# One-hots held twice: high and low parts of a matmul's second operand stacked on 128 rows in a four-layer graph network

## The chip, the cores and the metric

The kernel runs on one core of a Trainium2 chip. The metric is the device time in microseconds (us) of one execution. TensorE (PE in the profile) multiplies, VectorE (DVE), ScalarE (ACT) and GpSimd (POOL) work elementwise, and SyncE (SP) issues the DMAs. Matmul operands are mostly of type fp32r, a reduced form of float32[...]. To keep accuracy, a float32 operand is often split into a high part (rounded to fp32r) and a low part (the rest), and both are multiplied into the same sum.

## The reference

`x` has 8 batches of 2048 nodes with 64 channels, so a tile of 128 nodes is 128 x 512 numbers. Four layers follow each other, each as `x = layernorm(x + layer(x))`: a Chebyshev graph convolution with weights per node (layer 0), a hypergraph attention (layer 1), a graph convolution with two weights (layer 2), and one with normalized adjacency (layer 3). All use the same adjacency. Layer 1 is what matters here:

```
h = x @ W
alpha = softmax(where(H.T > 0, leaky_relu(h @ a_node), NEG))
agg = alpha @ h                                  # per hyperedge (64 of them)
beta = sigmoid((h @ a_gn)[:, None] + (agg @ a_ge)[None, :])
all_he = elu(beta * h[:, None] + (1 - beta) * agg[None, :])   # every node, every edge
coefs1 = softmax(where(H > 0, attn_scores(elu(agg)), NEG))    # over the edges of a node
g = sum over edges of coefs1 * all_he
industry = (adj / deg) @ (x @ W_ind)
coefs2 = softmax of attn_scores of (industry, g);  out = their mixture
```

A node lies in few of the 64 hyperedges: one drawn for it, and each other with a chance of 3%. The kernel uses that. Instead of all 64 edges it takes, for each node, its first, second and third edge, and a fourth list for what is left over. "The agg of this node's u-th edge" is then a product of a one-hot matrix (edges x nodes) with `agg` (edges x 512).

## The kernel before

**First product** (0 to 151 us). TensorE multiplies the adjacency with `x`, high and low (L471), while the lists of layer 1 are prepared beside it by the generator `memberships` (L295). For each quarter of the nodes (512 columns) VectorE makes two tiles of one-hots. `oh01` has the one-hots of the first edge on rows 0 to 63 and of the second edge on rows 64 to 127. `oh23` has those of the third edge and of the left-over list in the same way. They are stored in DRAM (L362, L400), along with `S` (which places left-over memberships) and `pT`. The working memory of this stage is then used again by layer 0, whose loads `srow` and `et` at 149 us wait for it.

**Layer 0** (151 to about 716 us) does the second product with the adjacency and the sums over node weights.

**Layer 1, preparation** (716 to 745 us, L511 on). `pT`, `oh01`, `S` and `oh23` are loaded whole, 128 x 2048 for the one-hots, on SyncE's queue (L541 to L544). `agg` is finished; its 64 edges stand twice, on rows 0 to 63 and on rows 64 to 127. The function `halves` makes a high and a low tile of `agg + 1` (`agg_hi`, `agg_lo`) and of `-agg` (`nagg_hi`, `nagg_lo`). The last step is a reciprocal on VectorE (L614), whose result `hgr` the loop needs. The temporary tiles of this part are in a pool `fa`, which is closed after it.

**Layer 1, loop** (745 to 1058 us). Four generators do the work of a node tile in small steps:

- `units(j)` (L643) is the attention of tile j. `sx` (L649) multiplies the one-hots with sums of `agg`, two matmuls of 32 columns in plain float32; then come `S` with `hgr` (L653) and a transpose. `gp0` and `gp1` (L696) fetch the agg rows of edges 1 and 2, and of edge 3 and the left-over list. Each is four matmuls on 64 rows: u = 0 high, u = 0 low, u = 1 high, u = 1 low. VectorE works on the result in `z0` and `z1` (L706, L710, L714), then exponential (L716) and minimum and maximum (L735). `dp` (L721, L723) is for the left-over list: `S` with `h`, then two 64-row matmuls with `nagg`. The result buffer of gp exists once.
- `industry(j)` is the product of the adjacency's mask with `x @ W_ind`: 32 matmuls of 128 rows and 512 columns into one accumulator (L1353), in groups of four, each group a step `p.i`. Its 1 MB mask tile `mj` is loaded on SyncE (L1348) into one of two buffers. `dlt` (L766) reads the accumulator and frees it for the next tile's first matmul.
- `mix_and_norm(j)` mixes, with transposes (`trm`), `fc` (L801) and `df` (L810), and normalizes.
- `layer2_steps` makes layer 2's features, `u` (L866), from each finished tile; most of them run after the loop, 1058 to 1095 us.

The order is written out by hand in the string `turns` (L894): one turn holds steps of six tiles, and begins with `q.ind u.gp0 u.z0 q.dlt m.xg m.tr0`, and later has `p.i u.w0 u.gp1 v.ST p.i`. `program_order()` makes TensorE, VectorE, ScalarE and GpSimd keep that order. SyncE's order is set by a scheduler: each DMA stands in its queue and waits there for the memory that it writes, and those behind it wait too. Nodes' tiles in memory come from pools that are stacked on each other, so the address of a later pool depends on the size of earlier ones.

**Layers 2 and 3** (1095 to 1363 us). Layer 2's product `a` (L1353 as well) loads the mask tiles again, into three buffers of a new pool `mj2`; that pool opens after layer 1's pools have closed, and so lies in memory that they used.

Of the kernel before, what the change touches and what calls it, by code (L numbers as in the profile page):

```python
# [8 lines left out]
F32 = mybir.dt.float32  # L9
# [3 lines left out]
ALU = mybir.AluOpType  # L13
AX = mybir.AxisListType
# [4 lines left out]
P = 128  # L19
NT = N // P  # L20
NQ, QW = 4, 512
NP = B // 2
BC = B * C
# [23 lines left out]
def r_(ap):  # L47
    return ap.bitcast(F32R)
# [3 lines left out]
def kernel(  # L52
# [56 lines left out]
    def b_view(t2):  # L109
        return t2.rearrange("p (b c) -> p b c", b=B)  # L110
# [118 lines left out]
    def lists_flag(box, tot, pm, w, an, avc):  # L229
# [53 lines left out]
    s_row = scr.tile([1, N], F32, tag="s_row", name="s_row")  # L283
    lists = {
        k: [scr.tile(shape, F32, tag=f"{k}{q}", name=f"{k}_{q}") for q in range(NQ)]
        for k, shape in (
            ("oh01", [P, QW]), ("oh23", [P, QW]), ("S", [P, 4, P]), ("pT", [E, QW])
        )
    }
    kept_i = [  # L290
        [scr.tile([P, BC], F32, tag=f"i{j}_{k}", name=f"kept_i_{j}_{k}") for k in range(2)]
# [3 lines left out]
    def memberships(pre, ps, pm, fcw_sb, fcb_sb, fcg_sb):  # L295
# [24 lines left out]
            pre.tile([P, NT], F32, tag=k, name=k) for k in ("cnt3", "base3", "end3")  # L320
        )
        raws = {}

        def load(q):
            raws[q] = pre.tile([P, QW], F32, tag="pT_raw", name=f"pT_raw_{q}")
# [20 lines left out]
        for q in range(NQ):  # L346

            raw = raws.pop(q)
            pT = pre.tile([P, QW], F32, tag="pT", name=f"pT_{q}")
            nc.vector.tensor_scalar(r_(pT), raw, 0.0, None, op0=ALU.is_gt)  # L350
            nc.sync.dma_start(lists["pT"][q], pT[0:E])
            yield
            pf = ps.tile([P, QW], F32, tag="li", name=f"pf_{q}")
            nc.tensor.matmul(
                pf, r_(tri.rearrange("p h e -> p (h e)")), r_(pT[0:E]), start=True, stop=True
            )
            yield
            pfm = raw
            nc.vector.tensor_tensor(pfm, pf, pT, ALU.mult)
            oh01 = pre.tile([P, QW], F32, tag="oh01", name=f"oh01_{q}")  # L360
            nc.vector.tensor_scalar(r_(oh01), pfm, order01, None, op0=ALU.is_equal)
            nc.sync.dma_start(lists["oh01"][q], oh01)  # L362
            oh23 = pre.tile([P, QW], F32, tag="oh23", name=f"oh23_{q}")
            nc.vector.tensor_scalar(r_(oh23[0:64]), pfm[0:64], 3.0, None, op0=ALU.is_equal)
            if q + 1 < NQ:
                load(q + 1)
            S = pre.tile([P, 4, P], F32, tag="S", name=f"S_{q}")
            yield
            for t in range(4):
# [26 lines left out]
                yield  # L396
                nc.vector.tensor_tensor(
                    r_(oh23[64:128, cols]), sm[64:128, P:2 * P], iota[64:128, 1, :], ALU.is_equal
                )
            nc.sync.dma_start(lists["oh23"][q], oh23)  # L400
            nc.sync.dma_start(lists["S"][q], S)
            yield

# [107 lines left out]
    def layer1(  # L511
# [7 lines left out]
        l1 = stack.enter_context(tc.tile_pool(name="fl1", bufs=1))  # L519

        oh01 = l1.tile([P, N], F32, tag="oh01", name="oh01")
        oh23 = l1.tile([P, N], F32, tag="oh23", name="oh23")

        S = l1.tile([P, NT, P], F32, tag="S", name="S")

        agg_hi, agg_lo = (
            l1.tile([P, BC], F32, tag=f"agg{i}", name=f"agg_{i}") for i in range(2)
        )  # L530
# [4 lines left out]
        ext = l1.tile([P, 2, 2, B], F32, tag="ext", name="ext")  # L535

        with tc.tile_pool(name="fa", bufs=2) as fa:
            pT = fa.tile([E, N], F32, tag="pT", name="pT", bufs=1)
            for q in range(NQ):
                cols = slice(q * QW, (q + 1) * QW)  # L540
                nc.sync.dma_start(pT[:, cols], lists["pT"][q])  # L541
                nc.sync.dma_start(oh01[:, cols], lists["oh01"][q])
                nc.sync.dma_start(S[:, 4 * q:4 * q + 4, :], lists["S"][q])
                nc.sync.dma_start(oh23[:, cols], lists["oh23"][q])  # L544
            stage1 = ExitStack()
            ps_tr, ps_mm = (
                stage1.enter_context(tc.tile_pool(name=n, bufs=k, space=PSUM))
# [2 lines left out]
            with program_order():  # L550
# [2 lines left out]

                he = fa.tile([P, BC], F32, tag="xT", name="he")
                nc.scalar.activation(he, agg, AF.Exp)
                nagg_hi, nagg_lo = (
                    own.tile([P, BC], F32, tag=f"b0_{k}", name=f"nagg_{k}") for k in (11, 15)
                )

                def halves(hi, lo, f, c):  # L560
                    s = slice(0 if c else 64, P)
                    nc.vector.tensor_scalar(r_(hi[s]), agg[s], f, c, op0=ALU.mult, op1=ALU.add)
                    full = fa.tile([P, BC], F32, tag="full", name="full", bufs=1)
                    nc.vector.tensor_scalar(full[s], agg[s], f, c, op0=ALU.mult, op1=ALU.add)
                    nc.vector.tensor_tensor(r_(lo[s]), full[s], hi[s], ALU.subtract)

                nc.vector.tensor_scalar(he, he, 1.0, -1.0, op0=ALU.min, op1=ALU.add)
                nc.vector.tensor_tensor(he, he, agg, ALU.max)
# [2 lines left out]
                    transpose(tr[:, pr, :], he[:, pr * P:(pr + 1) * P])  # L571
                heT = fa.tile([P, NP * P], F32, tag="hs", name="heT", bufs=3)
                nc.scalar.copy(heT, tr.rearrange("p r c -> p (r c)"))
                halves(agg_hi, agg_lo, 1.0, 1.0)
                fc = ps_mm.tile([P, 2, QW], F32, tag="mm", name="fche")
                for h in range(2):
                    rs = slice(h * 64, (h + 1) * 64)
# [4 lines left out]
                    b_view(he), b_view(agg),  # L582
                    vecs[:, 2, :].unsqueeze(1).to_broadcast([P, B, C]), ALU.mult,
                )
                nc.gpsimd.memset(ext, 0.0)
                sp = ps_tr.tile([P, QW], F32, tag="sm", name="sep")
                for b in range(B):
                    nc.tensor.matmul(
# [12 lines left out]
                for j in range(NT):  # L601
# [4 lines left out]
                for h in range(2):  # L606
                    s = slice(h * 64, (h + 1) * 64)
                    nc.vector.tensor_reduce(ext[s, h, 0, :], b_view(he)[s], AX.X, ALU.add)
                    nc.vector.tensor_copy(ext[s, h, 1, :], ese[s])
# [31 lines left out]
        extv = ext.rearrange("p u k b -> p (u k b)")  # L641

        def units(j, dst):  # L643

            cols = slice(j * P, (j + 1) * P)
# [45 lines left out]
            for i in range(2):  # L691
                gp = ps_g.tile([P, 2, BC], F32, tag="g", name=f"gp_{j}_{i}")
                for u in range(2):
                    rs = slice(u * 64, (u + 1) * 64)
                    for part in (agg_hi, agg_lo):
                        nc.tensor.matmul(  # L696
                            gp[:, u, :], r_((oh01, oh23)[i][rs, cols]), r_(part[rs]),
                            start=part is agg_hi, stop=part is agg_lo,
                        )
# [18 lines left out]
                if i == 0:  # L718

                    dp = ps_m.tile([P, BC], F32, tag="m", name=f"dp_{j}")  # L720
                    nc.tensor.matmul(dp, S[:, j, :], h_sb[:, j, :], start=True, stop=False)  # L721
                    for part in (nagg_hi, nagg_lo):
                        nc.tensor.matmul(  # L723
                            dp, r_(oh23[64:128, cols]), r_(part[64:128]),
                            start=False, stop=part is nagg_lo,
                        )
# [1356 lines left out]
```

## Time and profile before

| | us |
|---|---|
| three runs | 1359.33, 1359.80, 1364.57 |
| median | 1359.8 |
| profiled execution | 1364.62 |
| its span in the profile | 1362.9 |

| part of the span | from | to |
|---|---|---|
| first product, with the lists | 0 | 151 |
| layer 0 | 151 | 716 |
| layer 1, preparation | 716 | 745 |
| layer 1, loop | 745 | 1058 |
| layer 2's features | 1058 | 1095 |
| layer 2 and layer 3 | 1095 | 1363 |

| in the loop, 889.39 to 906.82 us | |
|---|---|
| TensorE busy, 889.4 to 906.8 | 17.40 of 17.40 us |
| VectorE busy | 14.71 us |
| ScalarE busy | 10.84 us |
| GpSimd busy | 10.46 us |
| granted TensorE clock | 1.00 |

A line of a timeline has the start, the duration, the engine, the line of the kernel, the operation, what it writes and reads, and in brackets how long the engine idled before it and what ended the wait. "x4" is four instructions in a row. SPq is SyncE's queue: the time is that of the issue, not of the transfer. Matmuls overlap, so a matmul's duration is longer than the step to the next. The granted clock is 1.00 at full speed and 0.50 at half. In a table by stretches, each engine has its busy time and the number of its instructions; the three last columns are the granted clock, the share of DMA time and GB/s.

### The profile page before, as it was taken

How to read it: one execution, taken by the hardware profiler on the slowest of the kernel's cores; microseconds unless marked ns; L12 is line 12 of the kernel's file. 1: busy time of each engine (PE TensorE's matmuls, PEld its weight loads, DVE VectorE, ACT ScalarE, POOL GpSimd, SP SyncE). 2: the span in 40 equal slices, each digit the busy share in tenths (PEclk: the TensorE clock that was granted, in tenths of full speed). 3: DMA queues.
4: the chain of work that ended last, by engine and by line, in shares of the span. 5: the costliest groups of instructions: out<-in, count | busy, mean ns of one | idle time of the engine just before them, and what ended most of it. 6: DMA issues, size and time to landing. Idle time of an engine off the chain costs nothing.

```text
span 1362.9 us, 20154 instructions
## 1 busy us (share of the span) xinstructions
PE 1304.4 (96%) x7884; PEld 1019.4 (75%) x7884; DVE 919.2 (67%) x1611; ACT 370.7 (27%) x844; POOL 420.2 (31%) x353
## 2 busy tenths in 40 slices
PE   7999899999999999999986799999998899999997
PEld 6777688888888888888874466666665788888885
DVE  4555378787777777777663768888885656666454
ACT  3000101121112222222221345666665521111111
POOL 0000353444444444444210445666553510000000
PEclk9999899999999999999985788999998899999999
DMA  8865432333333333331604111222220223334552
GB/s 285 238 187 167 135 111 89 104 103 103 103 103 103 103 103 104 104 101 55 232 24 140 69 52 65 77 78 78 78 78 1 93 94 124 115 109 141 185 185 72
DMA packets 91047, 153.01 MB, mean 112 GB/s; under 512 B 12097, under 2 KB 55489, under 8 KB 84673
## 3 DMA queue, kind: packets, MB, share of 16 engines
q1 hardware_dynamic: 88642, 147.46, 32.4%
q10 hardware_dynamic: 2304, 4.20, 0.8%
q8 instruction: 64, 1.05, 0.3%
q14 instruction: 37, 0.30, 0.1%
HBM read 115.97 MB, written 35.66 MB: 111 GB/s over the span
## 4 chain that ended last, share of the span: by engine, by line
PE 92%; DVE 3%; ACT 2%; DMA 1%; issue 1%; POOL 0%; SPq 0%; ACTq 0%; DVEq 0%; POOLq 0%
PE pp L1081 25%; PE a L1353 17%; PE ind L1353 9%; PE y2p L1044 9%; PE y1p L471 9%; PE fc L801 3%; PE df L810 2%; PE gp L696 2%; PE trm L154 1%; PE yp L1441 1%; PE try L1017 1%; PE aggp L1190 1%; PE dp L721 1%; PE sgp L1138 1%; PE red L746 1%; PE u L866 1%
## 5 line engine op out<-in xcount | busy, mean ns | idle before, releaser
L1092 DVE SCALAR_TENSOR_TENSOR r<-pp,emb_sb,r 128x256 f32<-128x256 f32 x512 | 247.4, 483 | 123.5 <-PE pp L1081 109.8
L1081 PE MATMUL pp<-w_sb,xT 64*128 64x256 f32 x1024 | 160.4, 390 | 1.7 <-DVE r L1092 1.7
L1081 PE MATMUL pp<-w_sb,y1T 64*128 64x256 f32 x1024 | 153.5, 376 | 0.0
L1081 PE MATMUL pp<-w_sb,y2T 64*128 64x256 f32 x1024 | 153.5, 376 | 0.0
L1030 POOL TENSOR_TENSOR r<-xs,bn 128x256 f32<-128x256 f32 x32 | 22.6, 727 | 413.7 <-issue 263.0
L471 PE MATMUL y1p<-x_hi,m 128*128 128x512 f32 x256 | 106.7, 417 | 7.2 <-ACT x_hi L419 7.1
L1081 PEld LDWEIGHTS pp<-w_sb,xT 64*128 64x128 f32 x1024 | 94.4, 186 | 25.1 <-issue 14.9
L737 POOL TENSOR_TENSOR ez<-ez,coef 128x1024 f32<-128x1024 f32 x32 | 65.1, 2033 | 142.2 <-DVE ez L735 119.8
L1081 PEld LDWEIGHTS pp<-w_sb,y1T 64*128 64x128 f32 x1024 | 99.7, 187 | 10.9
L1081 PEld LDWEIGHTS pp<-w_sb,y2T 64*128 64x128 f32 x1024 | 99.6, 187 | 11.0
L1353 PE MATMUL ind<-y_hi,mj_l 128*128 128x512 f32 x256 | 106.2, 415 | 0.8 <-DVE dlt L766 0.7
L1044 PE MATMUL y2p<-y_hi,msk 128*128 128x512 f32 x256 | 103.7, 405 | 0.0
L471 PE MATMUL y1p<-x_lo,m 128*128 128x512 f32 x256 | 101.9, 398 | 0.0
L1353 PE MATMUL a<-y_hi,mj_l 128*128 128x512 f32 x256 | 101.3, 396 | 0.6 <-ACT y_hi L874 0.6
L1044 PE MATMUL y2p<-y_lo,msk 128*128 128x512 f32 x256 | 101.7, 397 | 0.0
L1353 PE MATMUL a<-y_lo,mj_l 128*128 128x512 f32 x256 | 101.2, 395 | 0.0
L1353 PE MATMUL ind<-y_lo,mj_l 128*128 128x512 f32 x256 | 100.9, 394 | 0.0
L1353 PE MATMUL a<-v_hi,mj_l 128*128 128x512 f32 x256 | 100.1, 392 | 0.0
L1353 PE MATMUL a<-v_lo,mj_l 128*128 128x512 f32 x256 | 99.9, 391 | 0.0
L994 POOL TENSOR_TENSOR ms<-msk,srow 128x1024 f32<-128x1024 f32 x32 | 89.9, 2811 | 5.7 <-DVE ms L1007 5.7
L1353 PEld LDWEIGHTS ind<-y_hi,mj_l 128*128 128x128 f32 x256 | 48.5, 190 | 33.7 <-issue 18.1
L986 DVE TENSOR_SCALAR msk<-adj 128x1024 fp32r<-128x1024 f32 x32 | 63.7, 2024 | 4.1 <-PE y1p L471 4.1
(269 smaller groups left out, 2413.6 us busy)
## 6 DMA issues: line engine op xcount, KB each, us to landing
mj_l<-mask SPq DMA_DIRECT2D x48, 1024.0 KB, 4.9
raw<-in_at SPq DMA_DIRECT2D x32, 512.0 KB, 5.1
adj<-in_at SPq DMA_DIRECT2D x64, 256.0 KB, 3.6
mask<-msk SPq DMA_DIRECT2D x32, 512.0 KB, 4.5
xraw<-in_xn SPq DMA_DIRECT2D x8, 512.0 KB, 5.6
oh<-oh SPq DMA_DIRECT2D x16, 256.0 KB, 3.7
xT<-in_xt SPq DMA_DIRECT2D x16, 256.0 KB, 2.9
xs<-in_xn SPq DMA_DIRECT2D x16, 256.0 KB, 2.8
```

The source lines that it names most:

```text
L471: nc.tensor.matmul(accs[q][jj], r_(m[:, t, jj * P:(jj + 1) * P]), r_(part[:, mt, :]), start=i + h + t == 0 and part is x_hi, stop=i == 3 a ...
L696: nc.tensor.matmul(gp[:, u, :], r_((oh01, oh23)[i][rs, cols]), r_(part[rs]), start=part is agg_hi, stop=part is agg_lo,)
L737: nc.gpsimd.tensor_tensor(by_b(ez), by_b(ez), per_b(coef, 2 * i, 2), ALU.mult)
L801: nc.tensor.matmul(fc[:, h, :], fcw_sb[rs], sT[rs], start=True, stop=True)
L810: nc.tensor.matmul(df[:, b:b + 1], th[:, b % 2, (b // 2) * P:(b // 2 + 1) * P], av_sb, start=True, stop=True,)
L986: nc.vector.tensor_scalar(r_(m), raws[j][h], 0.0, None, op0=ALU.is_gt)
L994: nc.gpsimd.tensor_tensor(ms, m, srow[j].unsqueeze(1).to_broadcast([P, 8, P]), ALU.mult)
L1030: nc.gpsimd.tensor_tensor(r[:, 4 * bq * C:4 * (bq + 1) * C] .rearrange("p (h l c) -> p h l c", h=2, l=2), swapped(terms[j]["xs"], bq), bn. ...
L1044: nc.tensor.matmul(acc, r_(msk[j, mt // 8][:, mt % 8, :]), r_(part[:, mt, :]), start=mt == 0 and part is y_hi, stop=mt == NT - 1 and part ...
L1081: nc.tensor.matmul(pp[:, h, pl, :], terms[j][name][rs, 2 * bq + pl], w_sb[rs, k, dq * 4 * C:(dq + 1) * 4 * C], start=k == 0, stop=k == K - 1,)
L1092: nc.vector.scalar_tensor_tensor(rb, ppv[:, :, dd, :], emb_sb[:, j, d:d + 1], rb, op0=ALU.mult, op1=ALU.add)
L1353: nc.tensor.matmul(acc, r_(a[:, mt, :]), r_(part[:, mt, :]), start=mt == 0 and part is hi, stop=mt == NT - 1 and part is lo,)
```

## The change

All in layer 1 and in the making of its lists:

- The stored one-hots have another layout. For each tile of 128 nodes there are four one-hot matrices `oh[:, u, :]`, and each of them stands twice, on rows 0 to 63 and on rows 64 to 127. The function `store` writes each half of a computed tile to both places. That is 8 DMAs of 128 KB for a quarter, in place of 2 of 256 KB.
- The loads of `oh01` and `oh23` in the preparation are gone, and their 16 KB a partition. `units` loads a tile of 128 x 4 x 128 (256 KB) for its own j, on SyncE, into one of four buffers (8 KB a partition in all).
- `agg1` replaces `agg_hi` and `agg_lo`: its rows 0 to 63 hold the high part and its rows 64 to 127 the low part. `nagg` and `ext` are made in the same way by `parts`. A matmul over all 128 rows then sums high and low by itself.
- gp0 and gp1 have two matmuls on 128 rows each, in place of four on 64. dp has one in place of two. sx has four fp32r matmuls of 16 columns in place of two float32 ones of 32.

```diff
+        def store(q, oh, first):
+            for h in range(2):
+                for u in range(2):
+                    nc.sync.dma_start(
+                        lists["oh"][q][h * 64:(h + 1) * 64, :, first + u, :],
+                        oh[u * 64:(u + 1) * 64].rearrange("e (t n) -> e t n", t=4),
+                    )
...
-            nc.sync.dma_start(lists["oh01"][q], oh01)
+            store(q, oh01, 0)
...
-            nc.sync.dma_start(lists["oh23"][q], oh23)
+            store(q, oh23, 2)
...
-        oh01 = l1.tile([P, N], F32, tag="oh01", name="oh01")
-        oh23 = l1.tile([P, N], F32, tag="oh23", name="oh23")
...
-                nc.sync.dma_start(oh01[:, cols], lists["oh01"][q])
-                nc.sync.dma_start(oh23[:, cols], lists["oh23"][q])
...
+                low = slice(64, P)
+                def parts(dst, full):
+                    nc.vector.tensor_copy(r_(dst), full)
+                    nc.vector.tensor_tensor(r_(dst[low]), full[low], dst[low], ALU.subtract)
+                def scaled_parts(dst, f, c):
+                    full = fa.tile([P, BC], F32, tag="full", name="full", bufs=1)
+                    nc.vector.tensor_scalar(full, agg, f, c, op0=ALU.mult, op1=ALU.add)
+                    parts(dst, full)
...
-                halves(agg_hi, agg_lo, 1.0, 1.0)
+                scaled_parts(agg1, 1.0, 1.0)
...
-                nc.gpsimd.memset(ext, 0.0)
...
-                halves(nagg_hi, nagg_lo, -1.0, 0.0)
+                scaled_parts(nagg, -1.0, 0.0)
...
+            oh = small("oh", f"oh_{j}", (P, 4, P), 4)
+            nc.sync.dma_start(oh, lists["oh"][j // 4][:, j % 4])
...
-            for i in range(2):
+            for u in range(4):
                 nc.tensor.matmul(
-                    sm[:, P + 32 * i:P + 32 * i + 32], (oh01, oh23)[i][:, cols], extv,
+                    sm[:, P + 16 * u:P + 16 * u + 16], r_(oh[:, u, :]), r_(extv),
                     start=True, stop=True,
                 )
...
                 for u in range(2):
-                    rs = slice(u * 64, (u + 1) * 64)
-                    for part in (agg_hi, agg_lo):
-                        nc.tensor.matmul(
-                            gp[:, u, :], r_((oh01, oh23)[i][rs, cols]), r_(part[rs]),
-                            start=part is agg_hi, stop=part is agg_lo,
-                        )
+                    nc.tensor.matmul(
+                        gp[:, u, :], r_(oh[:, 2 * i + u, :]), r_(agg1), start=True, stop=True
+                    )
...
-                    for part in (nagg_hi, nagg_lo):
-                        nc.tensor.matmul(
-                            dp, r_(oh23[64:128, cols]), r_(part[64:128]),
-                            start=False, stop=part is nagg_lo,
-                        )
+                    nc.tensor.matmul(dp, r_(oh[:, 3, :]), r_(nagg), start=False, stop=True)
```

More of the change, by code (lines that the diff above doesn't have):

```diff
@@ L285 @@
         k: [scr.tile(shape, F32, tag=f"{k}{q}", name=f"{k}_{q}") for q in range(NQ)]
-        for k, shape in (
-            ("oh01", [P, QW]), ("oh23", [P, QW]), ("S", [P, 4, P]), ("pT", [E, QW])
-        )
+        for k, shape in (("oh", [P, 4, 4, P]), ("S", [P, 4, P]), ("pT", [E, QW]))
     }
@@ L519, in layer1 @@
         l1 = stack.enter_context(tc.tile_pool(name="fl1", bufs=1))
-        oh01 = l1.tile([P, N], F32, tag="oh01", name="oh01")
-        oh23 = l1.tile([P, N], F32, tag="oh23", name="oh23")
         S = l1.tile([P, NT, P], F32, tag="S", name="S")
-        agg_hi, agg_lo = (
+        agg1, nagg = (
             l1.tile([P, BC], F32, tag=f"agg{i}", name=f"agg_{i}") for i in range(2)
@@ L534, in layer1 @@
         nc.vector.memset(mhalf, -0.5)
-        ext = l1.tile([P, 2, 2, B], F32, tag="ext", name="ext")
+        ext = l1.tile([P, 2, B], F32, tag="ext", name="ext")
         with tc.tile_pool(name="fa", bufs=2) as fa:
@@ L555, in layer1 @@
                 nc.scalar.activation(he, agg, AF.Exp)
-                nagg_hi, nagg_lo = (
-                    own.tile([P, BC], F32, tag=f"b0_{k}", name=f"nagg_{k}") for k in (11, 15)
-                )
-                def halves(hi, lo, f, c):
-                    s = slice(0 if c else 64, P)
-                    nc.vector.tensor_scalar(r_(hi[s]), agg[s], f, c, op0=ALU.mult, op1=ALU.add)
+                low = slice(64, P)
[3 more added lines that the diff above has]
+                def scaled_parts(dst, f, c):
                     full = fa.tile([P, BC], F32, tag="full", name="full", bufs=1)
-                    nc.vector.tensor_scalar(full[s], agg[s], f, c, op0=ALU.mult, op1=ALU.add)
-                    nc.vector.tensor_tensor(r_(lo[s]), full[s], hi[s], ALU.subtract)
+                    nc.vector.tensor_scalar(full, agg, f, c, op0=ALU.mult, op1=ALU.add)
+                    parts(dst, full)
                 nc.vector.tensor_scalar(he, he, 1.0, -1.0, op0=ALU.min, op1=ALU.add)
@@ L605, in layer1 @@
                     )
[L606 to L609, printed above, removed]
+                sums = fa.tile([P, 2, B], F32, tag="sums", name="sums", bufs=1)
+                nc.vector.tensor_reduce(sums[:, 0, :], b_view(he), AX.X, ALU.add)
+                nc.vector.tensor_copy(sums[:, 1, :], ese)
+                parts(ext, sums)
                 rec = fa.tile([P, NT, B], F32, tag="rec", name="rec", bufs=1)
@@ L640, in layer1 @@
         ps_fc = stack.enter_context(tc.tile_pool(name="ff", bufs=1, space=PSUM))
-        extv = ext.rearrange("p u k b -> p (u k b)")
+        extv = ext.rearrange("p k b -> p (k b)")
         def units(j, dst):
-            cols = slice(j * P, (j + 1) * P)
+            oh = small("oh", f"oh_{j}", (P, 4, P), 4)
+            nc.sync.dma_start(oh, lists["oh"][j // 4][:, j % 4])
             sm = ps_s.tile([P, QW], F32, tag="sm", name=f"sx_{j}")
-            for i in range(2):
+            for u in range(4):
                 nc.tensor.matmul(
-                    sm[:, P + 32 * i:P + 32 * i + 32], (oh01, oh23)[i][:, cols], extv,
+                    sm[:, P + 16 * u:P + 16 * u + 16], r_(oh[:, u, :]), r_(extv),
                     start=True, stop=True,
@@ L693, in units @@
                 for u in range(2):
-                    rs = slice(u * 64, (u + 1) * 64)
-                    for part in (agg_hi, agg_lo):
-                        nc.tensor.matmul(
-                            gp[:, u, :], r_((oh01, oh23)[i][rs, cols]), r_(part[rs]),
-                            start=part is agg_hi, stop=part is agg_lo,
-                        )
+                    nc.tensor.matmul(
+                        gp[:, u, :], r_(oh[:, 2 * i + u, :]), r_(agg1), start=True, stop=True
+                    )
                 yield f"gp{i}"
@@ L721, in units @@
                     nc.tensor.matmul(dp, S[:, j, :], h_sb[:, j, :], start=True, stop=False)
-                    for part in (nagg_hi, nagg_lo):
-                        nc.tensor.matmul(
-                            dp, r_(oh23[64:128, cols]), r_(part[64:128]),
-                            start=False, stop=part is nagg_lo,
-                        )
+                    nc.tensor.matmul(dp, r_(oh[:, 3, :]), r_(nagg), start=False, stop=True)
                     yield "dp"
```

## The prediction

> **What bounds the kernel now.** I read the page's busy table, then its chain, then costly groups and DMA issues.
>
> ```profile
> span 1362.9 us, 20154 instructions
> PE 1304.4 (96%) x7884; PEld 1019.4 (75%) x7884; DVE 919.2 (67%) x1611; ACT 370.7 (27%) x844; POOL 420.2 (31%) x353
> PE 92%; DVE 3%; ACT 2%; DMA 1%; issue 1%; POOL 0%; SPq 0%; ACTq 0%; DVEq 0%; POOLq 0%
> ```
>
> TensorE is busy 96% and carries 92% of the chain. The lines that the change shortens, L696 (2%) and L721/L723 (1%), are small in it. So I price four places one by one: end of the first product, start of layer 1's loop, the loop's turn, hand-over to layer 2.
>
> The turn: three timelines of 889 to 907 us (TensorE twice, VectorE between).
>
> ```profile
> 889.39 0.73 PE L696 MATMUL gp<-agg,oh 64*128 64x512 f32 x4
> 893.89 0.73 PE L723 MATMUL dp<-nagg,oh 64*128 64x512 f32 x2
> 894.62 0.50 PE L1353 MATMUL ind<-y_hi,mj_l 128*128 128x512 f32 x1
> 896.36 0.39 PE L1353 MATMUL ind<-y_lo,mj_l 128*128 128x512 f32 x1
> 896.67 0.73 PE L696 MATMUL gp<-agg,oh 64*128 64x512 f32 x4
> 897.34 0.50 PE L1353 MATMUL ind<-y_hi,mj_l 128*128 128x512 f32 x1
> 906.82 0.73 PE L696 MATMUL gp<-agg,oh 64*128 64x512 f32 x4
> ```
> ```profile
> 890.18 1.22 DVE L706 SCALAR_TENSOR_TENSOR d<-h,gp 128x1024 f32<-128x1024 f32 x1 [1.38 <-PE gp L696]
> 893.83 0.74 DVE L766 SCALAR_TENSOR_TENSOR dlt<-ind,sdeg,g 128x512 f32<-128x512 f32 x1
> ```
>
> A turn is 906.82 − 889.39 = 17.43 us. Its first part is set by VectorE: gp0 ends, three passes (L706, L710, L714) and dlt (L766) follow without a gap, and ind starts at 894.62, when dlt has ended (894.57). Meanwhile TensorE does trm, sx, fc and dp, and it too ends at 894.62: a tie. From there on TensorE streams to the next gp0.
>
> The two other places, from the timelines around 745 and 1081 to 1096 us:
>
> ```profile
> 744.38 0.95 DVE L614 RECIPROCAL hgr<-rec 128x128 f32<-128x128 f32 x1
> 746.22 1.23 PE L696 MATMUL gp<-agg,oh 64*128 64x512 f32 x4
> ```
> ```profile
> 1081.25 1.27 SPq L1348 DMA_DIRECT2D mj_l<-mask  x3
> 1093.64 1.16 PE L866 MATMUL u<-w_sb,xT 64*128 64x128 f32 x16 [0.42 <-DVE y_lo L876]
> 1095.43 0.47 PE L1353 MATMUL a<-y_hi,mj_l 128*128 128x512 f32 x1 [0.63 <-ACT y_hi L874]
> ```
>
> The loop begins right behind a reciprocal, with its one-hots long in memory. Layer 2's first masks are issued at 1081.25, 14 us before product a needs them: hidden.
>
> [...] In stretches of 1 us (the 0.69 below is the granted clock, so that it fell to 0.5 after 0.38 us) it fell at 797.38, 817.86 and 961.22, which are 6.0 and 42.0 windows apart, and came back after 2, 2 and 1 windows.
>
> ```profile
> 797.00:798.00 1.00, 1.00 (x10) 1.00 (x8) 1.00 (x1) 0.59 (x1) 1.00 (x1) 0.69 0.99 418
> 817.00:818.00 1.00, 1.00 (x11) 0.79 (x8) 0.66 (x1) 0.51 (x2) 0.92 (x3) 0.93 0.91 385
> 961.00:962.00 1.00, 1.00 (x4) 0.43 (x4) 0.96 (x2) 0.06 (x1) 1.00 (x2) 0.61 0.94 385
> ```
>  [...] one 128-row matmul starts 0.227 us after another (0.427 at half clock), while four half-row ones of a gp, two on each half, take 0.67: three such steps, so they overlap in part only. [...] a 256 KB tile (xs, xr) landed 2.6 us after issue at the least, 2.8 and 3.2 at the median.
>
> **Part by part.**
>
> *Stores in the first product.* 32 DMAs of 128 KB take the place of 8 of 256 KB. SyncE's issue of one is 0.33 to 0.4 us, so 24 × 0.4 = about 10 us more over 150 us of a queue that mostly waits for VectorE. In 20 to 148 us TensorE's waits for raw or adj loads don't appear, which is the cover; uncovered, it would be up to that 10. In the program's order no load moves behind a store by more than its slack. At the end it shows: the last oh store is issued at 146.22, landed 149.11, srow waits for it (its memory is reused) at 149.20, and TensorE idled 0.58 for srow at 152.70. Two stores now end there: one more issue (0.4) and a little for 512-byte pieces: **+0.6** (0 to +1.5).
>
> *Preparation, 716 to 745 us.* The bulk load of one-hots (2 MB) goes; pT and S land earlier, but the reciprocal hangs on matmuls and VectorE, not on them. VectorE's splitting stays alike in number (a copy for a second scaling), and ext comes after the critical operations: 0 (−0.5 to +0.5).
>
> *Loop start.* Layer 1's first mj loads now wait only for layer 0's last matmul and move from 745.46 to about 722. But the four oh tiles lie in memory of the preparation's pool and wait for the reciprocal: queued behind each other on SyncE are oh_0 to oh_3, and behind oh_0 waits the whole loop. Issue 745.4, landing 2.8 later: 748.2. Then sx (four matmuls, 0.86 at half clock, the records before) and S with the transpose (745.39 to 746.22 = 0.83), so gp0 starts at 749.9 to 750.1, not 746.22. gp0 itself is 0.2 shorter, so VectorE's z0 moves by about **+3.7** (3.3 to 4.5). Everything until the first ind (767.3) follows z0.
>
> *The turn.* gp0 becomes two full-row matmuls; VectorE can start after 0.23 + 0.39 = 0.62 instead of 0.73: −0.11. dp (one instead of two, −0.3 or so) and sx (four 16-column matmuls) lie beside VectorE's passes and only make TensorE wait for dlt, some 0.5 us: worth nothing. gp1 stands in the streaming part: from the ind before it to the second after it is 897.67 − 896.36 = 1.31, and will be 4 × 0.23 = 0.92: −0.39. No one waits later for it: VectorE reaches z1 at 897.55, when gp1 is done. So −0.50 a turn, 16.93 in place of 17.43; × 14 = −7.0. The filling turn and unit 0 at half clock are bound by TensorE: −1.2 and −0.2. Loop: **−8.4** (−4 to −10).
> The oh load of a later tile waits for the unit that frees its buffer, three turns ahead, and adds 256 KB to 1.25 MB a turn at a DMA share of 0.2: 0. Without that lead each would cost the 2.8 of a landing.
>
> *Hand-over.* With one-hots gone from layer 1's pool, pools lie elsewhere, and in the changed program mj of layer 2's tile 0 waits for the last u matmul (L866, tile 15), xT and rstd; before, for rstd alone. Two more mj loads queue behind it. Its issue goes from 1081.25 to 1093.64 + 1.16 = 1094.8. A 1 MB load landed in 4.6 us at the least, so a starts at about 1099.7 instead of 1095.43: +4.3. After 4.9 us idle the clock will be half: a window of 8 to 14 matmuls at 0.427 instead of 0.227 is +1.6 to +2.8, taken as 2.1 (the first 14 of y2p at 153.28 were so slowed). **+6.4** (+4 to +9).
>
> *Sum:* 0.6 + 3.7 − 8.4 + 6.4 = +2.3. The profiled execution took 1364.6 (span 1362.9 and 1.7 around it), so its like would take 1366.9. It lies near the top of the three runs (1359.3 to 1364.6); at the median 1359.8 the forecast is **1362.1**.
>
> **Rivals.** Half a per cent, 6.8 us, is what a measurement of this kernel can tell from no change: bounds 1353.0 and 1366.6.
>
> *A. More half-clock spells: slower.* The three spells made their turns 3.1, 3.1 and 1.7 us longer, 7.9 in all. Each window that tripped began within 0.5 us of df's start: it held df (one-column matmuls), gp, transposes and sx, the thinnest stretch. The change thins it further (gp 0.67 to 0.46). And the turn nears five windows (17.07): it slid 0.36 a turn against the grid, and will slide 0.14 the other way, so once near a bad phase it stays longer, although a spell itself shifts the phase. At 2.6 each, two spells more than before already decide: +5.2 gives 1367; four give 1372. As many fewer give 1357. Against it: most turns showed no spell.
>
> *B. The hand-over stays hidden:* if I misread whose memory the load takes, +2.3 − 6.4 = −4.1: 1355.7. For: before, the same load went out 12 us ahead of the last u. Against: its wait now names that u.
>
> *C. gp1's 0.39 is filled by another wait,* for instance gp1 being held by the exponential's reader (TensorE's weights waited 0.4 for ez, L735, here). Only −0.11 a turn and the filling's −1.4 stay: loop −2.9, total +7.8: 1367.6. Against: gp1's start moves with gp0, by −0.11, and its length is still saved.
>
> *D. Full-row matmuls save dp's time too,* if dlt isn't the setter: −0.4 more a turn, −5.6: 1356.5. Against: dlt ends 0.05 before ind.
>
> **How the numbers follow.** The sum as it stands 0.53; A 0.23; B 0.07; C 0.11; D 0.06. The likeliest case alone spans 1357 to 1367 (terms' bounds, and 5 us between runs). A and C end beyond 1366.6 mostly, the sum's upper edge in a seventh: 0.23 × 0.85 + 0.11 × 0.7 + 0.53 × 0.15 = 0.35. B and D give faster in about a third (0.04), the sum's lower edge, with fewer spells, in 0.03: 0.07 in all. The range 1355 to 1372 leaves out some 0.1 on either side.
>
> **What would show it.** gp0 to gp0 at 16.93 us, with TensorE waiting about 0.5 for dlt at each ind; gp as two records 0.23 apart; sx waiting for DMA oh at 748; mj of layer 2 issued near 1095 on the new scale and the first a waiting for it by some 4 us at a clock of 0.5; bp waiting about 1.2 for srow. Turns of 17.3 would show C right, of 16.5 D. Spells counted by the clock decide A. Wrong above all would be: no wait at layer 2's first a, or spells in turn after turn.

## The result and the profile after

The change makes no difference that can be measured. The changed kernel took 1360.39 us (median of 12 runs, 1357.42 to 1362.95), the kernel before 1360.07 (12 runs, 1357.60 to 1370.35). The ratio is 0.9989, with a 95% interval of 0.9970 to 1.0009. It is formed from all runs and not from the two medians; four of the twelve runs of the kernel before took 1364 to 1370 us. The forecast was 1362.1, with a chance of 0.58 for a time within half a per cent of the kernel before (what 0.35 for slower and 0.07 for faster leave).

The page of the changed kernel, its span, busy table and chain:

```profile
span 1358.8 us, 20038 instructions
PE 1282.6 (94%) x7804; PEld 1020.2 (75%) x7804; DVE 917.2 (68%) x1611; ACT 370.4 (27%) x844; POOL 420.4 (31%) x352
PE 87%; DVE 8%; ACT 2%; DMA 2%; issue 1%; SPq 0%; POOL 0%; ACTq 0%; DVEq 0%; POOLq 0%
```

TensorE lost 21.8 us of busy time, and the span only 4.1. The chain shows what came in its place: VectorE went from 3% to 8%, since VectorE's passes now end alone before ind, and DMAs from 1% to 2%.

The turn, TensorE's timeline of the changed kernel:

```profile
864.67 0.71 PE L698 MATMUL gp<-agg,oh 128*128 128x512 f32 x2
868.51 0.79 PE L723 MATMUL dp<-agg,oh 128*128 128x512 f32 x1
869.87 0.50 PE L1350 MATMUL ind<-y_hi,mj_l 128*128 128x512 f32 x1 [0.57 <-DVE dlt L763]
881.64 0.71 PE L698 MATMUL gp<-agg,oh 128*128 128x512 f32 x2
```

A turn is 881.64 − 864.67 = 16.97 us (17.43 before), and TensorE idles 0.57 us for dlt at each. The start of the loop, timeline at 744 us:

```profile
743.70 0.95 DVE L615 RECIPROCAL hgr<-rec 128x128 f32<-128x128 f32 x1
744.79 1.74 SPq L649 DMA_DIRECT2D oh<-oh  x4
748.56 0.99 PE L653 MATMUL sx<-ext,oh 128*128 128x16 f32 x4 [5.78 <-DMA oh<-oh]
749.94 1.20 PE L698 MATMUL gp<-agg,oh 128*128 128x512 f32 x2
```

The four loads go out when the reciprocal has ended, the first has landed 3.8 us later (sx starts), and gp0 starts 5.29 us after the reciprocal's end (0.89 before). The hand-over to layer 2, timeline at 1083 us:

```profile
1083.01 1.16 PE L863 MATMUL u<-w_sb,xT 64*128 64x128 f32 x16 [0.42 <-DVE y_lo L873]
1084.32 1.27 SPq L1345 DMA_DIRECT2D mj_l<-mask  x3
1089.14 0.77 PE L1350 MATMUL a<-y_hi,mj_l 128*128 128x512 f32 x1 [4.97 <-DMA mj_l<-mask]
1089.70 0.63 PE L1350 MATMUL a<-y_lo,mj_l 128*128 128x512 f32 x1
1090.13 0.63 PE L1350 MATMUL a<-y_hi,mj_l 128*128 128x512 f32 x1
```

The mask load is issued behind the last u, and a waits 4.97 us for it. From the second on, its first matmuls step by 0.43 us and not 0.23: half clock. The granted clock fell to 0.50 at 1087.21, 3.0 us into TensorE's wait, and was 1.00 again from 1094.04.

The two spans as a ledger, each row a difference between two marks of the two timelines. A clock window is the measured grid of the granted clock: in both traces every interval between two changes of it is a whole multiple of 3.413 us, the length of the shortest spell (961.23 to 964.64 in the kernel before). A half-clock spell is one such window, or several in a row, at a granted clock of 0.50. The first three turns, in which the loop fills, are called filling turns, the twelve that follow up to gp0 of tile 15 steady turns.

| stretch | after minus before, us |
|---|---|
| to the first bp | +0.61 |
| first bp to the end of the reciprocal | −1.29 |
| reciprocal to gp0 of tile 0 | +4.40 |
| gp0 of tile 0 to gp0 of tile 15, half-clock spells left out | −8.51 |
| the loop's half-clock spells (7.80 before, 2.37 after) | −5.43 |
| gp0 of tile 15 to the last u | −0.41 |
| last u to first a (1.79 before, 6.13 after) | +4.34 |
| first a to the end | +2.19 |
| sum (1362.9 to 1358.8) | −4.1 |

The spells are counted from the steady turns: 20.54, 20.55 and 19.00 us in place of 17.43 before; one of 19.34 in place of 16.97 after.

### The profile page after: what moved, and what is told of

Same layout as the page of the kernel before. It is cut to its first block, busy times and chain, and to the rows that moved or that the text cites. A ratio compares the mean times of both kernels' runs of the same rounds, so it can differ in the third digit from the quotient of the medians.

```text
span 1358.8 us, 20038 instructions
## 1 busy us (share of the span) xinstructions
PE 1282.6 (94%) x7804; PEld 1020.2 (75%) x7804; DVE 917.2 (68%) x1611; ACT 370.4 (27%) x844; POOL 420.4 (31%) x352
## 4 chain that ended last, share of the span: by engine, by line
PE 87%; DVE 8%; ACT 2%; DMA 2%; issue 1%; SPq 0%; POOL 0%; ACTq 0%; DVEq 0%; POOLq 0%
PE pp L1078 25%; PE a L1350 17%; PE ind L1350 9%; PE y2p L1041 9%; PE y1p L478 9%; PE df L807 2%; PE fc L798 2%; DVE d L711 1%; DVE d L715 1%; DVE d L707 1%; PE gp L698 1%; PE yp L1438 1%; PE try L1014 1%; PE aggp L1187 1%; PE sgp L1135 1%
## 5 line engine op out<-in xcount | busy, mean ns | idle before, releaser
L1078 PEld LDWEIGHTS pp<-w_sb,y1T 64*128 64x128 f32 x1024 | 99.7, 187 | 10.9
L478 PEld LDWEIGHTS y1p<-x_hi,m 128*128 128x128 f32 x256 | 48.9, 191 | 20.2 <-ACT x_hi L426 7.2
```

The lines of the kernel that those rows point to most:

```text
L478: nc.tensor.matmul(accs[q][jj], r_(m[:, t, jj * P:(jj + 1) * P]), r_(part[:, mt, :]), start=i + h + t == 0 and part is x_hi, stop=i == 3 a ...
L1078: nc.tensor.matmul(pp[:, h, pl, :], terms[j][name][rs, 2 * bq + pl], w_sb[rs, k, dq * 4 * C:(dq + 1) * 4 * C], start=k == 0, stop=k == K - 1,)
```

## Experiments

The theory: the two waits for loads (start, hand-over) eat what the loop gains, and both come from where the change puts tiles in memory. The rivals: the gain in the loop is something else, or it is all a matter of half-clock spells.

**The start.** oh gets a pool of its own, opened last, so that it lies behind the memory of the preparation's temporary pool:

```diff
         fw = stack.enter_context(tc.tile_pool(name="fw", bufs=2))
         mjp = stack.enter_context(tc.tile_pool(name="mj1", bufs=2))
+        ohp = stack.enter_context(tc.tile_pool(name="ohp", bufs=4))
...
-            oh = small("oh", f"oh_{j}", (P, 4, P), 4)
+            oh = ohp.tile([P, 4, P], F32, tag="oh", name=f"oh_{j}")
```

> The changed kernel, with the tiles oh in a pool of their own behind layer 1's mask buffers, so that their memory is not that of the preparation's pool. My theory: oh_0 to oh_3 then wait only for layer 0's last matmul and land long before the reciprocal; gp0 of tile 0 starts about 1 us after the reciprocal ends (as before the change, 0.9) and not 5.3 after it (as in the changed kernel); the hand-over to layer 2 keeps its wait of some 5 us. So -4.2 us against the changed kernel: about 1356. Rival: the start is set by something else (the mask tiles of layer 1, which now wait for the reciprocal again and land at about 750, or VectorE's order), and the gain is under 1 us.

Measured: 1354.40 us (17 runs), 0.9950 of before (0.9929 to 0.9972); the kernel before, run beside it, took 1359.34 (27 runs). Timeline of this kernel at the same place:

```profile
721.96 1.74 SPq L650 DMA_DIRECT2D oh<-oh  x4
742.16 1.02 PE L654 MATMUL sx<-ext,oh 128*128 128x16 f32 x4
743.15 0.95 DVE L615 RECIPROCAL hgr<-rec 128x128 f32<-128x128 f32 x1
744.23 0.80 SPq L1346 DMA_DIRECT2D mj_l<-mask  x2
744.71 1.20 PE L699 MATMUL gp<-agg,oh 128*128 128x512 f32 x2
```

The loads go out 22 us earlier, sx is done ahead of the reciprocal, and gp0 starts 0.61 us after its end. Now the mask loads wait for the reciprocal, and nothing waits for them. First a still waits 5.09 us for its mask. The theory's step holds; the rival (masks or VectorE's order) falls. The time is 6.0 under the changed kernel's of the first measurement and not 4.2; 0.7 of it lies between the two measurements (the kernel before took 1360.07 and 1359.34).

**The hand-over.** Layer 1's mask buffers are put ahead of the work pool in memory. By the theory, layer 2's masks then lie on layer 1's fixed tiles and masks, and no longer touch the work pool, whose last tile (xT) is read by the last u. The traces show no addresses, only what a load waits for:

```diff
-        fw = stack.enter_context(tc.tile_pool(name="fw", bufs=2))
         mjp = stack.enter_context(tc.tile_pool(name="mj1", bufs=2))
+        fw = stack.enter_context(tc.tile_pool(name="fw", bufs=2))
```

> The changed kernel, with layer 1's mask buffers ahead of its work pool in memory, so that layer 2's mask buffers lie on the former and on layer 1's fixed tiles and not on the work pool. My theory: the first mask load of layer 2 waits for the last ind and the last rstd only, goes out some 10 us before the first a, which follows the last u by about 0.6 us instead of 5, and at full clock. The start of the loop keeps its wait for oh. So -4.3 for the wait and -2.2 for the clock: about 1354. Rival: a wait of some other thing (the casts of the last features) holds the first a nearly as long, and only the load is earlier: less than 1 us.

Measured: 1351.46 us (9 runs), 0.9923 of before (0.9897 to 0.9949). In its timeline the load goes out 12 us before the last u, and a follows at once, at full clock:

```profile
1067.45 29.31 SPq L1345 DMA_DIRECT2D mj_l<-mask  x5
1079.82 1.16 PE L863 MATMUL u<-w_sb,xT 64*128 64x128 f32 x16 [0.42 <-DVE y_lo L873]
1081.61 0.47 PE L1350 MATMUL a<-y_hi,mj_l 128*128 128x512 f32 x1 [0.63 <-ACT y_hi L871]
```

Wait and clock are gone as expected. The time is 8.9 us under the changed kernel's of the first measurement, and not 6.5; 0.7 of it lies between the two measurements. Its profiled execution had no half-clock spell in the loop, where the changed kernel's had one (2.4).

**Both moves.** The two edits together: masks, work pool, then oh.

> The changed kernel with both moves of memory. My theory: the two gains are in different places and add: -4.2 and -6.5 to about 1349.7, 0.992 to 0.993 of the time before the change, which is the loop's gain of 8 to 9 us with a little lost in the first product's stores. Rival: the two kernels differ in the number of half-clock spells and not in these waits; then the times of all three kernels of this call lie within 3 us of the changed kernel, in no order.

Measured: 1351.39 us (8 runs, 1347.18 to 1351.97), 0.9930 of before (0.9901 to 0.9958). The two waits are gone in the trace (gp0 starts 0.61 us after the reciprocal's end, and a idles 0.63 for its cast, as before the change), but the medians don't add. Two things had come in. The first is the turn: 17.03 us and not 16.97, in both versions with the masks at the other place. The second is the clock. Its profiled execution, at a mean granted clock of 0.969, took 1347.2; the other seven, at 0.963 to 0.966, took 1349.7 to 1352.0. By each run's own mean clock the picture is orderly. On a straight line of time over clock through each kernel's runs, at 0.965, before comes to 1359.6, the changed kernel to 1359.4, the start alone to 1354.3 and both to 1350.9. The runs of the hand-over alone lie at 0.967 to 0.970. On the same lines at 0.967, the changed kernel comes to 1357.8, the start alone to 1352.6, the hand-over alone to 1353.1 and both to 1349.4. So at one clock the moves give 5.2 and 4.7, and together 8.4; the turn of 17.03 takes 0.7 of the rest. The rival of this run (only spells) falls: the kernels are 5 and 9 us apart at the same clock. Part of it stood, though: spells move a median by some us.

**The loop's parts.** The changed kernel with one thing put back to 64 rows each time. For gp a tile `aggc` with high and low swapped holds the other operands, and for dp a tile `nagg_hi`. The first diff is that for gp0; for gp1 its condition is `i == 1`:

```diff
-                    nc.tensor.matmul(
-                        gp[:, u, :], r_(oh[:, 2 * i + u, :]), r_(agg1), start=True, stop=True
-                    )
+                    if i == 0:
+                        rs = slice(u * 64, (u + 1) * 64)
+                        for k in range(2):
+                            part = (agg1, aggc)[(u + k) % 2]
+                            nc.tensor.matmul(
+                                gp[:, u, :], r_(oh[rs, 2 * i + u, :]), r_(part[rs]),
+                                start=k == 0, stop=k == 1,
+                            )
+                    else:
+                        nc.tensor.matmul(
+                            gp[:, u, :], r_(oh[:, 2 * i + u, :]), r_(agg1),
+                            start=True, stop=True,
+                        )
```

```diff
-                    nc.tensor.matmul(dp, r_(oh[:, 3, :]), r_(nagg), start=False, stop=True)
+                    for part in (nagg_hi, nagg):
+                        nc.tensor.matmul(
+                            dp, r_(oh[64:128, 3, :]), r_(part[64:128]),
+                            start=False, stop=part is nagg,
+                        )
```

> The changed kernel with only gp0 put back to four 64-row matmuls (a second tile with high and low parts swapped holds their operands; gp1, dp and sx stay on 128 rows). My theory: gp0 is followed by VectorE's passes, so the turn grows by the later end of gp0 alone, 0.11 us, from 16.97 to 17.08, and TensorE's wait for dlt before ind stays near 0.4. Rival (matmul time counts wherever it stands): +0.2 or more, to 17.17. The preparation has two more passes of VectorE, about 1 us, which is not the question.

> The changed kernel with only gp1 put back to four 64-row matmuls. My theory: gp1 stands in the part of the turn where TensorE streams, so its whole difference of 0.39 us comes back: the turn goes from 16.97 to 17.36, gp0 to gp1 stays at 7.16. Rival (another wait had filled the gain): under 0.2. The preparation has two more passes of VectorE, about 1 us.

> The changed kernel with only dp put back to two 64-row matmuls with high and low part of -agg. My theory: dp lies beside VectorE's passes, so TensorE's wait for dlt shrinks from 0.57 to about 0.15 and the turn stays at 16.97. Rival: dlt is not what sets ind, and the turn grows by 0.4 to 17.4. The preparation has one more pass of VectorE, about 0.5 us.

Measured in one execution each (1359.44, 1366.01 and 1358.12 us), by the median of the steady turns: gp0 on half rows 17.05 us, gp1 17.35, dp 16.96, where the changed kernel has 16.97. TensorE's timeline of a turn of the kernel with gp0 on half rows, then of that with gp1, then of that with dp:

```profile
897.07 1.84 PE L821 MATMUL df<-av_sb,th 128*128 128x1 f32 x16
898.84 0.49 PE L706 MATMUL gp<-agg,oh 64*128 64x512 f32 x1
898.84 0.72 PE L706 MATMUL gp<-aggc,oh 64*128 64x512 f32 x2
899.18 0.39 PE L706 MATMUL gp<-agg,oh 64*128 64x512 f32 x1
906.03 0.62 PE L711 MATMUL gp<-agg,oh 128*128 128x512 f32 x2
915.88 0.50 PE L706 MATMUL gp<-agg,oh 64*128 64x512 f32 x1
```
```profile
920.02 0.71 PE L711 MATMUL gp<-agg,oh 128*128 128x512 f32 x2
927.27 0.49 PE L706 MATMUL gp<-agg,oh 64*128 64x512 f32 x1
937.38 0.71 PE L711 MATMUL gp<-agg,oh 128*128 128x512 f32 x2
```
```profile
904.08 1.02 PE L726 MATMUL dp<-h,S 128*128 128x512 f32 x2
905.04 0.49 PE L728 MATMUL dp<-nagg_hi,oh 64*128 64x512 f32 x1
905.90 0.50 PE L1358 MATMUL ind<-y_hi,mj_l 128*128 128x512 f32 x1
```

gp1 gives back 0.38, gp0 0.08 and dp nothing: it uses up TensorE's wait for dlt (0.57 in the changed kernel, none shown here, where 0.15 was expected to stay). Together 0.46, the whole difference of the turns. A rival for so small a number as 0.08 is the place in memory, since the added tile moves what lies behind it, and a turn of 17.03 came with another place in the two kernels above. It doesn't hold: there the ind matmuls stepped more slowly (0.233 us), and here they step as in the changed kernel (0.230 us). sx was not put back alone. So what a matmul is worth depended on where it stands: 0.38 for one gp, 0.08 for the same gp elsewhere. The four half-row matmuls also show their pairs: one on each half starts at the same time (898.84), and the two pairs are 0.34 apart. So four on two halves take two steps of 0.34, and two on all rows two of 0.23.

**The two moves in another way.** Six buffers for oh, opened ahead of the preparation's pool; the masks stay behind the work pool:

```diff
+        ohp = stack.enter_context(tc.tile_pool(name="ohp", bufs=6))
         with tc.tile_pool(name="fa", bufs=2) as fa:
...
-            oh = small("oh", f"oh_{j}", (P, 4, P), 4)
+            oh = ohp.tile([P, 4, P], F32, tag="oh", name=f"oh_{j}")
```

> Both moves of memory made in another way: six buffers for oh, in a pool opened ahead of the preparation's pool, so that oh's memory is free early and layer 2's masks lie on it and on the fixed tiles; layer 1's masks stay behind the work pool, as in the changed kernel. In the runs with the masks of layer 1 ahead of the work pool, the turn was 17.03 and not 16.96, as each matmul after a high part began 0.233 and not 0.227 us after it; 17.03 is nearly five clock windows (17.07). My theory: the turn is 16.96 again, so against the version with both moves -0.8 us and another number of half-clock spells; both waits are gone as in it: 1347 to 1351. Rival: the slower step comes with something else of those versions, the turn is 17.03, and the time is within 1 us of that version's 1351.4.

Measured: 1349.37 us (5 runs, 1347.74 to 1351.41), 0.9935 of before (0.9921 to 0.9948; before 1358.86). The turn is 16.95, so the slower one had come with those other places in memory. In the runs with the masks ahead of the work pool, ind matmuls stepped by 0.233 us in the mean, here by 0.230; the place of the masks is the difference that these versions have in common, but which operand's address does it was not tried. The time is 11.0 us under the changed kernel's of the first measurement, of which 1.2 lies between the two measurements; the ledger's rows for the two waits and the clock behind them sum to 4.40 + 4.34 + 2.19 = 10.9. (Side by side, both with df moved as below, the difference is 9.2.)

**The half-clock spells.** In the nine traces up to here there are 117 places where df stands ahead of a gp0, 13 in each trace from gp0 of tile 3 on, and the clock fell at 10 of them. All 10 are those at which a clock window began between 0.34 us before df and 0.47 after; none of the others tripped, the nearest at 0.39 before and 0.53 after. (In the trace with both moves, one more fell behind the last gp0, where no gp0 follows df: its window began 0.42 before df.) So the spell points to what is in that window: df, gp0, trm and sx. The changed kernel's spell, granted clock by stretches of 1 us (engines' busy times, then clock, DMA share, GB/s), and the df before it:

```profile
983.00:984.00 1.00, 1.00 (x9) 0.86 (x9) 0.00 (x0) 0.38 (x2) 1.00 (x2) 1.00 0.48 123
984.00:985.00 1.00, 1.00 (x10) 1.00 (x9) 0.81 (x1) 0.74 (x2) 0.92 (x3) 0.91 1.01 426
985.00:986.00 1.00, 1.00 (x5) 0.78 (x7) 0.97 (x2) 0.21 (x1) 1.00 (x1) 0.50 0.96 403
```
```profile
981.74 1.84 PE L807 MATMUL df<-av_sb,th 128*128 128x1 f32 x16
983.44 0.71 PE L698 MATMUL gp<-agg,oh 128*128 128x512 f32 x2
```

The clock falls at 984.82, so that the window ahead of it began at 981.41, 0.33 before df. TensorE counts as busy for the whole 3.41 us of this window, and of the three ahead of the kernel before's falls at 797.39, 817.87 and 961.23: busy time doesn't tell a dense stretch from a thin one. A test that needs no luck with phases: in `turns`, df goes ahead of the last four ind matmuls, in the kernel before, the changed one, and the last version.

```diff
-            "p.i o.centre p.i p.i m.th1 u.exp1 m.sub p.i v.gates u.e1 f.x2 v.tau s.g p.i o.sq "
-            "u.w1 m.df m.sw o.var"
+            "p.i o.centre p.i p.i m.th1 u.exp1 m.sub p.i v.gates u.e1 f.x2 v.tau s.g m.df p.i o.sq "
+            "u.w1 m.sw o.var"
```

> The kernel before the change, with df of a turn moved ahead of the turn's last four ind matmuls, so that df (one-column matmuls) and the next gp0 no longer stand side by side. Of the steady turns in the traces so far, the four in which a clock window began between 0.37 us before df and 0.42 after it were those that fell to half clock, and none of the others; 0.4 us of full matmuls at the window's edge were enough to escape. My theory (the loop's half-clock spells come from that thin stretch): no spell in the steady turns, a median some 3 us lower, 1355 to 1357, and no run of the list beyond 1364. Rival (spells come from the chip and have no place in the program): the same median and the same spread of 1356 to 1375, or a loss, as df now waits for VectorE.

> The changed kernel with the same move of df. My theory: it loses its fewer spells too, about 2 us, to 1357 to 1359; against the former run of this call it then shows what the change is worth without spells: start +3.7, loop -8.4, hand-over +6.4 and stores give about +1.5 us, between 0 and +3. Rival: the change's worth differs from this by more than 3 us, and the near-equality of the two kernels came from spells.

> The version with both waits removed (six buffers for oh, in a pool opened ahead of the preparation's pool), with the same move of df. My theory: 1349.4 less one spell of two windows or so, 1346 to 1348, with a spread of no more than 3 us. Rival: no different from 1349.4.

Measured side by side with the kernel before, which took 1359.11 (43 runs, 1355.89 to 1374.98):

| with df moved | us | runs, lowest to highest | ratio to before |
|---|---|---|---|
| the kernel before | 1355.44 | 22, 1352.78 to 1358.07 | 0.9961 (0.9940 to 0.9981) |
| the changed kernel | 1355.87 | 22, 1352.79 to 1358.65 | 0.9961 (0.9941 to 0.9982) |
| both waits removed | 1346.63 | 6, 1345.07 to 1346.92 | 0.9877 (0.9824 to 0.9929) |

No loop of the three traces has a spell in its steady turns (17.53 to 17.61 us, 16.95 to 17.05 and 16.94 to 17.05), though in 12 of these turns a window began between 0.34 us before df and 0.47 after. The tail up to 1375 us of the kernel before is gone; its highest of 22 is 1358.07. The rival (spells have no place in the program) falls. Between the first two, the change is worth +0.4 us, and with the waits removed −8.8. The move of df has a price of its own, though: in the kernel before the turn is 17.55 and not 17.43, which is 1.4 us over 12 steady turns, and in the changed kernel it stays at 16.97. Without that price, the change without spells would be worth about +1.8, as an estimate from these numbers. The changed kernel came out lower than the 1357 to 1359 expected. The last version beats both kernels.

## Why the prediction was right

The time is inside the range, 1.7 us under the forecast. The mechanism was right: a gain in the loop, and two waits, together of about its size, that the new places in memory bring, each found in the traces. The ledger without the spells and the −1.29 comes to +2.6, for a forecast of +2.3. That it fits so closely is in part luck, as two terms were right by misses that cancel or for another reason.

- *The turn.* Forecast −0.50, measured −0.46: gp1 −0.38 for −0.39, gp0 −0.08 for −0.11. Of gp0's part the forecast had the smaller piece: VectorE starts only 0.03 earlier (0.75 after gp0's start in place of 0.78). The larger one is the change-over from full to half rows, which I had not seen as a part of its own: gp0 starts 1.70 us after df (983.44 after 981.74 above), and 1.77 with gp0 on half rows (898.84 after 897.07). dp nothing, as said, with TensorE waiting 0.57 for 0.5. Loop without spells −8.51 for −8.4, and this is luck: the steady turns are fewer (12, not 14) and gave −5.6 for −7.0, the three filling turns −2.9 for −1.4. The filling turns' gain is likely in part one of clock. The half clock that the preparation leaves behind ended 19.8 us after gp0 of tile 0 and not 23.9; with dp or gp1 on half rows it ended 23.1 and 22.7 after, and the three turns took 48.2 and 48.4 us in place of 46.9. So dp is worth nothing in a steady turn alone, and how much of the filling's gain is clock was not separated.
- *Start of the loop.* The wait behind the reciprocal cost +4.40 and not +3.7: the first of four tiles landed in 3.8 us, not 2.8. That this is because they went out together is likely but was not tried. In the ledger it is partly hidden by the −1.29 ahead of it. That is no gain of the change, as far as these runs can tell: from the first bp to the end of the reciprocal took 592.6 us in the kernel before and 591.3 in the changed one, but 591.2 also in the kernel before with df moved, whose text is the same up to there.
- *Hand-over.* +4.34 for +4.3, and +2.19 for +2.1 of clock.
- *Stores.* +0.61 for +0.6, but not for the reason given. The issue of the two last stores took 0.57 and 0.62 us (one of 0.39 before), but they landed in 2.4 and 2.5 us and not 2.9, so srow was issued no later (149.14 and 149.20 before) and TensorE waited less for it (0.39, not the 1.2 that I named). Nor was a price of the 512-byte pieces shown here: over the whole stage a store of 128 KB landed in 2.8 us (median), one of 256 KB in 3.1. Two other things came in, and the runs don't separate them. From issue to the bp that waits for it, srow took 4.2 us and not 3.5. And TensorE's transposes ahead of bp began 0.41 later and ran partly at half clock. Their delay arises at 118 us, in TensorE's wait for VectorE's oh (first line before, the others after):

```profile
117.81 0.29 PE L374 MATMUL sm<-tri,pT 64*128 64x64 f32 x1 [0.38 <-DVE oh L397]
```
```profile
116.89 0.46 DVE L1329 TENSOR_TENSOR prod<-wb,vecs 64x64 f32<-64x64 f32 x2
117.39 0.46 DVE L1330 TENSOR_REDUCE wa<-prod 64x1 f32<-64x64 f32 x2
118.22 0.29 PE L381 MATMUL sm<-tri,pT 64*128 64x64 f32 x1 [0.85 <-DVE oh L404]
```

The added stores had pushed small loads of weights (wb, vecs) back on SyncE's queue, from 74 to 78 us to 100 to 113. VectorE's passes on them (80 to 85 us before) now stand in part right ahead of oh.
- *Rival A* (more spells) went the other way: one instead of three in the profiled executions, and of 12 runs each none over 1363.0, where the kernel before went up to 1370.4. The reading of where spells begin was right; TensorE counted as busy for all of the 3.41 us ahead of each of these four falls. What was wrong was the guess that a thinner gp0 would make them more frequent; what the turn of 16.97 did was to move the phase only 0.10 us a turn, and in the profiled execution it reached the bad place once, at the end.
- *Rivals B, C and D* fall by the first a's wait, by gp1 on half rows and by dp on half rows.

## What to carry to other kernels

A matmul saved is worth what the next wait leaves of it: the same gp gave 0.38 us where TensorE streams and 0.08 where VectorE's passes follow. When a change moves tiles between pools, read which memory each first load then reuses: here two loads lost their lead and cost 9 to 11 us, more than the loop's gain of 8.5, and a pool opened at another place gave it back. DMAs added to a queue can move the loads behind them (here wb and vecs, from 74 to 78 us to 100 to 113), and with these the work of another engine, to a worse place. Where runs of a kernel scatter by a per cent, compare their granted clocks (here 1355.89 us at a mean of 0.969, 1374.98 at 0.953) and look for a thin stretch on TensorE as long as the clock's grid in the trace (here 3.413 us).

## What the runs showed of the hardware

- In the traces of both kernels and of the three versions with df moved, the intervals between changes of the granted clock were whole multiples of 3.413 us. After a window with df (16 one-column matmuls, 1.8 us), gp0, trm and part of sx in it the clock was at 0.50, 10 times of 10; in the four of these in the traces of the two kernels TensorE was busy throughout (3.41 of 3.41 us). After a window that began 0.39 us before df, with full matmuls there, it stayed at 1.00, and so it did after each of 12 in which df stood between full matmuls.
- The same ind matmuls stepped by 0.233 us in the mean with the mask buffers ahead of the work pool in memory, and by 0.230 with them behind it; the turn was 17.03 us and 16.95 to 16.97.
- Going over to half-row matmuls cost 0.07 to 0.08 us at the change-over (gp1 started at 7.24 us of the turn and not 7.16, gp0 1.77 us after df and not 1.70), beside the longer group itself.
- In the kernel before, dp's `S` with `h`, a plain float32 matmul of 512 columns, left two records of 0.59 us each and took 0.95 us up to the next matmul (892.94 to 893.89); an fp32r one of 512 columns (ind) left one record and took 0.23.
